# GpSimd's order in an attention kernel: first difference, store, spread, key weights, a lead-in piece and the last additions

## The chip, the cores and the metric

The kernel runs on one core of a Trainium2 chip. The metric is the device time of one execution in microseconds, the median of several. A profiled execution gives the trace; its times are counted from the start of the span.

## What is computed

`x` has 2048 rows of 256. It is normalised (layernorm), and two things are added to it: an attention with 16 heads of 128 and no mask, and a feed-forward part whose weights are rounded to -1, 0 and 1.

```
xn = layernorm(x)
q, k, v = split(xn @ Wqkv.T)                      # 16 heads of 128 each
w   = softmax(q @ k.T / sqrt(128))                # 2048 x 2048 for each head
att = concat_over_heads(w @ v) @ Wout.T
ffn = ((sigmoid(xn @ Q(w1).T) * (xn @ Q(w2).T)) @ Q(w3).T)
x + att + ffn
```

Everything is float32.

## The kernel before

**Blocks and steps.** Layernorm, the feed-forward part and the first projections come first, in about 105 us. Then the kernel goes through 64 blocks: a block `n` is a head `h` and 512 of its queries (`b` from 0 to 3). A block has four steps `t` of 128 queries each. One loop (`u`) emits all steps, with the order on every engine written out by hand (`manual_schedule`): each engine runs its own instructions strictly in the order in which the loop emits them. The step that makes the scores runs `LEAD` = 6 steps ahead: step `u` makes the scores of step `v = u + 6` and uses the weights of block `n`, step `t`. The first six steps (`u < 0`) are the lead-in; pieces of the projections of heads 0 and 1 are placed in it by the table `first`, whose key is `v`.

**One step.** TensorE makes the scores of 128 queries in two halves of 1024 keys, in three score buffers (`scores`). VectorE takes the maximum (`mx`, `nm`); ScalarE the exponential of both halves into `p`, of which there are four buffers. `exchanged` then sends `p` in 16 DMAs of 64 KB to `part`, ten issued by SyncE (SP) and six by ScalarE; each moves 32 rows. Two steps later VectorE turns `part` in 32 by 32 blocks into the big tile `R` (`transposed`, line 644), where the keys lie along the partitions. ScalarE issues the six DMAs between two pairs of exponentials.

**The product with the values.** `R` has seven slots of 2048 columns, and a block uses five of them under the names a, b, c, d, e (`roles`). The product of weights and values is done by a scheme with seven instead of eight multiplications: `differences` (line 664, GpSimd) makes T1 = c - a into e, T2 = d - e into a, T3 = c = d - c, T4 = b = b - a. T1 and T3 come in two halves (a, b), T2 in two halves of key tiles (l, h), and T4 whole. `weighted(n, t, k)` (line 711, TensorE, tile `av`) uses b and a as they are in step 0, T1 and T2 in step 1, T3 in step 2, T4 in step 3. T2 overwrites a, so it waits for step 0's products; step 1's products wait for T2. `v_combined` makes four combinations of the values on GpSimd for each head, two ahead of a head's first block and two within it. `copied` (ScalarE, line 729) and `added` (VectorE, line 737) bring the pieces together in `oU`. `added` and the second read of a projection are held back in the list `behind` and emitted at the start of the next step.

**The row sums.** `inverses(n + 1)` in step 2 of block `n` makes the reciprocals of the row sums on VectorE and stores them to the chip's main memory as `rd` (line 615, GpSimd's queue). `spread(n)` (line 621, GpSimd's queue) brings them back to all partitions as `oT`, 256 KB. `added(n, 3)` multiplies `oU` by `oT` (line 741), and `put_away(n)` (line 767, GpSimd's queue) stores `oU` to `od`; this is the store of the title.

**Other transfers on GpSimd's queue** (`between`). Heads go in pairs `g`, eight blocks `i` each. In the first three blocks of a pair (but the first pair) the output projection of the pair before is added into a running sum: `y_moved` fetches 512 KB of the sum (`osums<-yd`) at the end of step 0 and stores another 512 KB (`yd<-osums`) in step 3, and `o_fetched` fetches 512 KB (`o<-od`) at the end of step 1. The weights of the next pair are loaded by `load_weights` (line 83): query and key weights, 256 KB each, while the scores of an even head's last block are made, value weights in step 1 of a pair's fourth block. `weight_sums` makes four small sums of them on GpSimd.

**The end.** The last block has no steps of its own: `last_weighted` multiplies its weights directly, in two parts, and the last projections (`projected`, `opened`) stand between.

The step's order on GpSimd comes from these lines: in step 0 `put_away(n - 1)`, T1b, `spread(n)`, T3b, T2l and `between`; in step 1 T2h, two of `v_combined`, T4 and `between`; in step 3 T1a and T3a of the next block, with `y_moved` between them.

Of the kernel before, what the change touches and what calls it, by code (L numbers as in the profile page):

```python
# [20 lines left out]
def layernorm_attention_bitffn_kernel(  # L21
# [14 lines left out]
    nc = tc.nc  # L36
# [9 lines left out]
    TB = QB // P  # L46
# [4 lines left out]
    G = 2  # L51
# [21 lines left out]
    def load_weights(g: int, what: str, queue=nc.sync):  # L73

        if what == "o":
            w = wpool.tile([P, G, DM], F32, tag="wvo", name=f"wo{g}")
            src = woutT[g * G * D : (g + 1) * G * D, :].rearrange("(h p) e -> p h e", p=P)
        else:
            tag = "wvo" if what == "v" else f"w{what}"
            w = wpool.tile([P, KC, G * D], F32, tag=tag, name=f"w{what}{g}")  # L80
            lo = "qkv".index(what) * HD + g * G * D
            src = wqkvT[:, lo : lo + G * D].rearrange("(c p) e -> p c e", p=P)
        queue.dma_start(w, src)
        weights[g, what] = w
# [136 lines left out]
    NV = NKT // 2  # L221
# [395 lines left out]
    def spread(n: int):  # L617

        if n < NBK - NB:
            r = rds[n % 2].rearrange("(j c) r -> j (c r)", c=32)[:, : TB * 32]  # L620
            nc.gpsimd.dma_start(
                oT.rearrange("p (j x) -> p j x", j=P // 32), r.partition_broadcast(P)
            )
            rbs[n] = oT
# [24 lines left out]
    def differences(n: int, what: str):  # L649

        a, b, c, d, e = roles[n]
        todo, where = what[:2], what[2:]
        o, x, y = {"T1": (e, c, a), "T2": (a, d, e), "T3": (c, d, c), "T4": (b, b, a)}[todo]
        o, x, y = (R[:, i] for i in (o, x, y))
        if where in ("a", "b"):
            t = "ab".index(where)
            o, x, y = (i[:, t * S // 2 : (t + 1) * S // 2] for i in (o, x, y))
        elif where in ("l", "h"):
            k = "lh".index(where)
            o, x, y = (  # L660
                i.rearrange("p (t k q) -> p t k q", t=2 * NQ, q=32)[:, :, k * KH // 2 : (k + 1) * KH // 2]
                for i in (o, x, y)
            )
        nc.gpsimd.tensor_tensor(o, x, y, ALU.subtract)  # L664
# [99 lines left out]
    def put_away(n: int):  # L764

        h, b = blocks[n]
        nc.gpsimd.dma_start(ods[h // G % 2][b][:, h % G], oU)  # L767
# [60 lines left out]
    def projected(n: int, u: int, pool=ps_m, tag: str = "m"):  # L828
# [34 lines left out]

    first = {
        1: [("v", 0, NV - 1), ("k", 1, 0)], 2: [("k", 1, 1), ("q", 0, NB - 1)],
        3: [("k", 1, 2), ("q", 1, 1)], 4: [("k", 1, 3), ("q", 1, 2)], 5: [("v", 0, NV - 2)],
    }
    made = {("q", 1, 0)} | {p for todo in first.values() for p in todo}

# [28 lines left out]
    behind = []  # L898
    with tc.manual_schedule():
        for u in range(-LEAD, (NBK - 1) * TB):  # L900
            n, t = divmod(u, TB)
            v = u + LEAD
            lead_in = u < 0
            more = v < NBK * TB
            h, b = blocks[v // TB] if more else (H, 0)


            seven = 2 <= h + 1 < H and v % TB < 2
            hi = h + 1, b, v % TB
            product, read, twice = fast_product, fast_read, (b % 2, v % TB) != (1, 1)  # L910


            g, i = divmod(n, GB)
            if n >= NB and t < 2:
                i, j = divmod(i, NB)
                j = 2 * j + t
                if not i:
                    seven, hi = True, (g - 1, j)
                    product, read, twice = o_product, o_read, False
                elif g + 1 < H // G:  # L920
                    seven, hi = True, (g + 1, j)
                    product, read, twice = v_product, v_read, False
            pms = []

            def beside():
                if v == 0:

                    for c, f in chunks[-2:]:
                        summed(fp, c, f)
                if seven:  # L930
                    pms.append(product(*hi, False))
                    read(*hi, False, pms[0])

            if behind:
                behind.pop()()
            if t == 0 and n >= 0:
                if 0 < n <= NBK - NB:
                    put_away(n - 1)
                differences(n, "T1b")
                spread(n)  # L940
                differences(n, "T3b")
            elif t == 1 and n >= 0:
                differences(n, "T2h")
                if blocks[n][1] == 0:
                    v_combined(blocks[n][0], 2)
                    v_combined(blocks[n][0], 3)
                differences(n, "T4")
            elif t == 3 and -1 <= n < NBK - 2:
                differences(n + 1, "T1a")
                if n % GB < NB <= n < NBK - NB - 2:  # L950
                    y_moved(n % GB, True)
                differences(n + 1, "T3a")
                if n >= 0 and blocks[n + 1][1] == 0:
                    v_combined(blocks[n + 1][0], 0)
                    v_combined(blocks[n + 1][0], 1)
            if more:
                scores(v, late=beside)

            if lead_in:
                for what, hg, i in first.get(v, ()):  # L960
                    {"q": q_piece, "k": k_piece, "v": v_piece}[what](hg, i)
                if v == 1:
                    front.close()
                    apool = ctx.enter_context(tc.tile_pool(name="apool", bufs=2))
                    oT = apool.tile([P, QB], F32, tag="oT", name="oT", bufs=1)
                    oU = apool.tile([P, QB], F32, tag="oU", name="oU", bufs=1)
                    R = apool.tile([P, 7, S], F32, tag="R", name="R", bufs=1)
                    for c in range(0, NB, 2):
                        x_sums(c)
            elif t == 1 and n > NBK - NB:  # L970
                projected(n - 1, 0)
            if n >= NBK - NB and t in (0, 3):

                opened(n - NBK + NB, t // 3, *((ps_m, "m") if more else (ps_s, "s")))
            if h == 0:
                if v % TB == 0 and ("k", 1, b) not in made:
                    k_piece(1, b)
                elif v % TB == 1 and ("q", 1, b) not in made:
                    q_piece(1, b)
            if b == NB - 1 and h + 2 < H:  # L980
                if h % G == 0 and v % TB in (0, 2):
                    load_weights(h // G + 1, "qk"[v % TB // 2], nc.gpsimd)
                if v % TB == 3:
                    weight_sums(h + 2)
            twice = seven and twice
            if t == 2 and -1 <= n < NBK - 1:
                inverses(n + 1)
            if v > 1 and v - 2 < NBK * TB - 2:
                transposed(v - 2)
            if u >= 0:  # L990
                for k in range(units[t]):
                    weighted(n, t, k)
            if twice:
                pms.append(product(*hi, True))
            if u >= 0:
                copied(n, t)

            def left(n, t, twice, read, hi, h, b, v, product, pms, seven):
                if n >= 0:
                    added(n, t)  # L1000
                if twice:
                    read(*hi, True, pms[1])

            behind.append(partial(
                left, n, t, twice, read, hi, h, b, v, product, pms, seven
            ))
            if more:
                exchanged(v)
            if v == NBK * TB + 1:
                transposed(v - 3)  # L1010
                transposed(v - 2)
            if t == 2 and n > NBK - NB:
                projected(n - 1, 1)
            if u == -1:
                v_combined(0, 0)
                v_combined(0, 1)
            if u >= 0:
                if t == 0:
                    differences(n, "T2l")
                between(n, t)  # L1020

        n = NBK - 1
        behind.pop()()
        for k in range(NKT):
            last_weighted(k, 0)
            if k in (KQ - 1, 3 * KQ - 1):
                projected(n - 1, k // (2 * KQ), ps_s, "s")
            elif k == 2 * KQ - 1:
                opened(NB - 1, 0, ps_s, "s")
        for k in range(NKT):  # L1030
            last_weighted(k, 1)
            if k == KQ - 1:
                opened(NB - 1, 1, ps_s, "s")
                projected(n, 0, ps_m, "m")
        projected(n, 1, ps_s, "s")
# [38 lines left out]
```

## Time and profile before

| | us |
| --- | --- |
| median of 3 runs | 2227.57 |
| lowest, highest | 2225.85, 2231.21 |
| the profiled execution | 2229.07 |
| its span in the trace | 2227.3 |

| engine | busy us | what most of it is |
| --- | --- | --- |
| TensorE (PE) | 2178.7 | scores 936.2, products with values 541.2 and 476.5 |
| VectorE (DVE) | 1726.2 | maxima 619.6, transposes 605.3 |
| GpSimd (POOL) | 1471.9 | differences 1176.4 |
| ScalarE (ACT) | 744.0 | exponentials 565.8 |

| GpSimd's instruction | us on GpSimd | us from issue to landing, median |
| --- | --- | --- |
| half a difference, 128x1024 | 2.367 | |
| T4, 128x2048 | 4.545 | |
| a value combination, 128x512 | 1.28 | |
| spread `oT<-rd`, 256 KB | 0.778 | 5.6 |
| sums' store `od<-oU`, 256 KB | 0.568 | 3.1 |
| sum's fetch `osums<-yd`, 512 KB | 0.555 | 4.5 |
| o fetch `o<-od`, 512 KB | 0.571 | 4.6 |
| sum's store `yd<-osums`, 512 KB | 0.563 | 4.0 |
| key weights `wk`, 256 KB | 0.734 | 5.2 |

How to read the profile: PE is TensorE's matmul row, whose ends are modelled; PEld is its weight load; `ACTq` and `SPq` are DMA issues by ScalarE and SyncE. In the timeline a row has its start, its duration, the engine and line, the operation and its tiles, and in square brackets the engine's idle time before it and what ended that. Rows of the same kind are merged (x29 are 29 instructions). The windows view gives busy time of each engine in a stretch, and behind them the granted clock of TensorE (1.00 is full), the share of the DMA engines and GB/s.

### The profile page before, as it was taken

To read this page: it belongs to the slowest core of one execution; us is meant where nothing else is said; L and a number is where in the kernel's file an instruction comes from. 1 tells how busy PE (TensorE), PEld (TensorE's weight loads), DVE (VectorE), ACT (ScalarE), POOL (GpSimd) and SP (SyncE) were. 2 spreads that over 40 slices of the span, in tenths; PEclk is the share of its full clock that TensorE was granted. 3 is DMA by queue.
4 is the path that set the end of the run, shared out by engine and by line. 5 is a ranking of instruction groups with operands and counts; after the bars stand their busy time and mean duration, and the time that the engine had idled before them with its cause. 6 is when DMAs were issued, how large, how long until landed. Compare 5 with 4: busy or idle time off the path is not lost.

```text
span 2227.3 us, 41859 instructions
## 1 busy us (share of the span) xinstructions
PE 2178.7 (98%) x14074; PEld 1190.1 (53%) x14074; DVE 1726.2 (77%) x2338; ACT 744.0 (33%) x1390; POOL 1471.9 (66%) x884
## 2 busy tenths in 40 slices
PE   9999999999999999999999999999999999999998
PEld 6744545546665444445666444444454445665465
DVE  6567887877888788878788778877888878887774
ACT  5543333233333333323333233323333333332331
POOL 0067667867667776767677776677667668677662
PEclk9999999999999999999999999999999999999999
DMA  2166666776667766677667666677667776667763
GB/s 92 49 151 156 153 150 165 192 193 168 147 172 201 178 168 160 171 191 186 147 171 180 186 176 152 165 194 182 162 152 181 195 178 160 168 175 191 185 168 94
DMA packets 229928, 367.87 MB, mean 165 GB/s; under 512 B 70800, under 2 KB 76304, under 8 KB 229712
## 3 DMA queue, kind: packets, MB, share of 16 engines
q1 hardware_dynamic: 127664, 174.95, 30.5%
q10 hardware_dynamic: 74896, 101.94, 17.9%
q0 software_dynamic: 27152, 88.30, 16.7%
q8 instruction: 111, 1.82, 0.4%
q14 instruction: 105, 0.86, 0.1%
HBM read 61.93 MB, written 34.54 MB: 43 GB/s over the span
## 4 chain that ended last, share of the span: by engine, by line
PE 64%; DMA 14%; SPq 4%; POOL 4%; DVE 3%; issue 2%; ACT 2%; ACTq 1%; DVEq 0%
PE s L94 27%; PE av L711 24%; DMA part<-p 14%; PE pw L94 5%; PE pvw L94 4%; SPq L597 4%; POOL R L664 3%; PE pow L94 2%; ACT p L578 2%; ACTq L597 1%; DVE R L644 1%; DVE mx L568 1%; PE av L94 1%; DVE oU L741 1%; ACT oU L729 0%
## 5 line engine op out<-in xcount | busy, mean ns | idle before, releaser
L664 POOL TENSOR_TENSOR R<-R 128x1024 f32<-128x1024 f32 x441 | 1176.4, 2679 | 132.2 <-DVE R L644 91.0
L578 ACT ACTIVATE p<-s,nm 128x1024 f32<-128x1024 f32 x512 | 565.8, 1110 | 1343.8 <-DMA part<-p 958.6
L94 PE MATMUL s<-kT,qT 128*64 128x512 f32 x4000 | 936.2, 594 | 19.5 <-ACT p L578 19.4
L568 DVE TENSOR_REDUCE mx<-s 128x1 f32<-128x1024 f32 x512 | 619.6, 1222 | 292.9 <-PE s L94 279.6
L644 DVE STREAM_TRANSPOSE R<-part 128x1024 f32<-128x1024 f32 x512 | 605.3, 1220 | 40.8 <-DMA part<-p 37.3
L94 PEld LDWEIGHTS s<-kT,qT 128*64 128x64 f32 x4000 | 370.4, 137 | 455.6 <-issue 290.7
L711 PE MATMUL av<-R,v 128*64 128x256 f32 x3728 | 541.2, 380 | 0.1
L711 PE MATMUL av<-R,st 128*64 128x256 f32 x3024 | 476.5, 384 | 15.6 <-POOL R L664 12.3
L711 PEld LDWEIGHTS av<-R,v 128*64 128x64 f32 x3728 | 341.2, 137 | 164.4 <-issue 37.3
L711 PEld LDWEIGHTS av<-R,st 128*64 128x64 f32 x3024 | 296.9, 139 | 161.2 <-issue 38.2
L615 POOL DMA_DIRECT2D rd<-r x60 | 33.7, 562 | 234.2 <-DVE r L614 234.2
L767 POOL DMA_DIRECT2D od<-oU x60 | 34.1, 568 | 218.3 <-DVE oU L741 215.9
L737 DVE TENSOR_TENSOR oU<-av,oU 64x256 f32<-64x256 f32 x248 | 102.2, 412 | 68.0 <-ACT oU L729 65.6
L94 PE MATMUL pow<-o,wo 128*64 128x512 f32 x448 | 108.7, 593 | 3.5 <-DVE qT L197 3.4
L729 ACT COPY oU<-av 64x256 f32<-64x256 f32 x248 | 90.7, 366 | 62.2 <-PE av L711 58.3
L94 PE MATMUL pvw<-wv,xnT 128*64 128x256 f32 x896 | 110.6, 379 | 0.0
L578 ACT ACTIVATION_READ_ACCUMULATOR p<-s,nm 128x1 f32 x512 | 100.3, 196 | 0.0
L94 PE MATMUL pw<-t,ws 128*64 128x512 f32 x336 | 98.0, 592 | 0.0
L94 PEld LDWEIGHTS pvw<-wv,xnT 128*64 128x64 f32 x896 | 69.7, 137 | 50.9 <-issue 16.0
L200 DVE TENSOR_TENSOR kT<-pw,kT 128x512 f32<-128x512 f32 x112 | 76.9, 686 | 1.8
L160 POOL TENSOR_TENSOR t<-xnT 128x512 f32<-128x512 f32 x4 | 5.1, 1267 | 106.8 <-DMA part<-p 106.8
L94 PEld LDWEIGHTS pow<-o,wo 128*64 128x64 f32 x448 | 38.3, 137 | 62.5 <-issue 43.0
(145 smaller groups left out, 1302.6 us busy)
## 6 DMA issues: line engine op xcount, KB each, us to landing
part<-p SPq DMA_DIRECT2D x2556, 64.0 KB, 2.3
part<-p ACTq DMA_DIRECT2D x1540, 64.0 KB, 2.3
oT<-rd POOLq DMA_DIRECT2D x60, 256.0 KB, 5.6
od<-oU POOLq DMA_DIRECT2D x60, 256.0 KB, 3.1
o<-od POOLq DMA_DIRECT2D x28, 512.0 KB, 4.6
osums<-yd POOLq DMA_DIRECT2D x28, 512.0 KB, 4.5
yd<-osums POOLq DMA_DIRECT2D x26, 512.0 KB, 4.0
yd<-yT SPq DMA_DIRECT2D x4, 512.0 KB, 2.6
```

The lines of the kernel that those rows point to most:

```text
L94: nc.tensor.matmul(out[c * HP : (c + 1) * HP], lhs[:, c * HP : (c + 1) * HP], rhs, start=start, stop=stop, skip_group_check=True,)
L200: nc.vector.tensor_tensor(k, pk, base, ALU.add)
L568: nc.vector.tensor_reduce(mx[:, i : i + 1], s, AX.X, ALU.max)
L578: nc.scalar.activation(p, s, AF.Exp, bias=nm, scale=SCALE, accum_out=sums[n][:, t, i : i + 1],)
L597: queue.dma_start(parts[v][g // 2][bass.ts(j, 32), g % 2, :], ps[j // 2][bass.ts(g, 32), bass.ts(j % 2, S // NQ)],)
L615: nc.gpsimd.dma_start(rds[n % 2], riT)
L644: nc.vector.transpose(to[:, t % 2, 2 * i : 2 * i + 2], part.rearrange("p g (s c) -> p g s c", s=2),)
L664: nc.gpsimd.tensor_tensor(o, x, y, ALU.subtract)
L711: nc.tensor.matmul(av[i * HP : (i + 1) * HP, half], l[:, kk], moving(s, kk), start=start, stop=(k == units[r] - 1), skip_group_check=True,)
L729: nc.scalar.copy(u[op, oq], av[ap, half])
L737: nc.vector.tensor_tensor(u[p, q], av[p, half], u[p, q], ALU.add)
L767: nc.gpsimd.dma_start(ods[h // G % 2][b][:, h % G], oU)
```

## The change

Five edits, all of them in the order in which instructions are emitted; no instruction is added or removed.

1. T1b is emitted ahead of `put_away(n - 1)` instead of behind it.
2. `spread(n)` moves from step 0, between T1b and T3b, to step 1, behind T2h. In the pair's first three blocks the sum's fetch, at the end of step 0, now comes ahead of it, and the o fetch, at the end of step 1, still behind it.
3. The next pair's key weights are loaded one step of `v` earlier: behind T3a in step 3, where before they stood behind T3b in step 0 of the next block. The query weights stay.
4. In the lead-in the last v piece goes from `v` = 5 to 4 and the last k piece from 4 to 5.
5. The additions of the last full step (`added(62, 3)`) are emitted ahead of the last four transposes on VectorE instead of behind them.

GpSimd's order of a block is then T1a, T3a | T1b, store, T3b, T2l | T2h, spread, T4.

```diff
     first = {
         1: [("v", 0, NV - 1), ("k", 1, 0)], 2: [("k", 1, 1), ("q", 0, NB - 1)],
-        3: [("k", 1, 2), ("q", 1, 1)], 4: [("k", 1, 3), ("q", 1, 2)], 5: [("v", 0, NV - 2)],
+        3: [("k", 1, 2), ("q", 1, 1)], 4: [("v", 0, NV - 2), ("q", 1, 2)], 5: [("k", 1, 3)],
     }
...
             if t == 0 and n >= 0:
+                differences(n, "T1b")
                 if 0 < n <= NBK - NB:
                     put_away(n - 1)
-                differences(n, "T1b")
-                spread(n)
                 differences(n, "T3b")
             elif t == 1 and n >= 0:
                 differences(n, "T2h")
+                spread(n)
...
             if b == NB - 1 and h + 2 < H:
-                if h % G == 0 and v % TB in (0, 2):
-                    load_weights(h // G + 1, "qk"[v % TB // 2], nc.gpsimd)
+                if h % G == 0 and v % TB in (0, 1):
+                    load_weights(h // G + 1, "qk"[v % TB], nc.gpsimd)
...
             if v == NBK * TB + 1:
+                behind.pop()()
                 transposed(v - 3)
                 transposed(v - 2)
...
         n = NBK - 1
-        behind.pop()()
         for k in range(NKT):
```

## The prediction

> **What bounds the kernel now.** I read the page first, then who waited for whom, then the timeline at each place where TensorE stood idle. The page says which engine sets the time:
>
> ```profile
> PE 2178.7 (98%) x14074; PEld 1190.1 (53%) x14074; DVE 1726.2 (77%) x2338; ACT 744.0 (33%) x1390; POOL 1471.9 (66%) x884
> ```
>
> TensorE (PE) is the bound. GpSimd (POOL) is busy two thirds of the time, so reordering it pays only where PE stands still for it. The view of waits, PE alone, gives those places (us, times, longest):
>
> ```profile
> PE s L94 <- ACT p L578: 19.4, 21, 3.1
> PE av L711 <- POOL R L664: 12.3, 12, 2.8
> ```
>
> Twelve waits for a difference, 12.3 us, are what this order can remove. The 19.4 us are scores that wait for a score buffer which ScalarE frees late; those are the danger. The timeline around block 0, then block 2, shows two of the twelve (start, duration, engine, line, idle before and its releaser):
>
> ```profile
> 141.37 1.27 POOL L686 TENSOR_TENSOR st<-v 128x512 f32<-128x512 f32 x1 [2.60 <-ACT v L242]
> 146.26 0.78 POOL L621 DMA_DIRECT2D oT<-rd  x1
> 151.78 5.14 PE L711 MATMUL av<-R,st 128*64 128x256 f32 x29 [2.55 <-POOL R L664]
> ...
> 205.41 0.58 POOL L767 DMA_DIRECT2D od<-oU  x1 [0.84 <-DVE oU L741]
> 211.43 0.73 POOL L83 DMA_DIRECT2D wk<-in_wqkvT_dram  x1
> 212.18 9.26 POOL L664 TENSOR_TENSOR R<-R 128x1024 f32<-128x1024 f32 x3
> 214.59 6.35 PE L711 MATMUL av<-R,st 128*64 128x256 f32 x29 [2.85 <-POOL R L664]
> ```
>
> PE waits for T2 in both, and the matmuls after the wait run slowly: 29 took 5.14 and 6.35 us, where elsewhere 32 take 3.45 us, that is 3.13 for 29. The windows view gives the reason (the column after POOL is the granted clock):
>
> ```profile
> 152.00:156.00 4.00, 4.00 (x24) 2.34 (x22) 2.37 (x2) 1.93 (x3) 4.00 (x3) 0.57 0.58 142
> ```
>
> A wait of 2.55 us is paid for again in clock. A steady block, then the first heavy block of a pair of heads, where the key weights come in between:
>
> ```profile
> 1023.79 0.58 POOL L767 DMA_DIRECT2D od<-oU  x1 [3.90 <-DVE oU L741]
> 1026.69 0.78 POOL L621 DMA_DIRECT2D oT<-rd  x1
> 1027.49 11.64 POOL L664 TENSOR_TENSOR R<-R 128x1024 f32<-128x1024 f32 x4
> ...
> 997.87 0.73 POOL L83 DMA_DIRECT2D wk<-in_wqkvT_dram  x1
> 1003.95 0.44 PE L711 MATMUL av<-R,st 128*64 128x256 f32 x2 [0.60 <-POOL R L664]
> ```
>
> In a steady block GpSimd idles 3.90 us, then stores, takes T1b, the spread, T3b and both T2 halves in one go, and PE (from 1034.75) just finds them ready. One more issue of 0.73 us in that run costs PE 0.60. Last, the tail:
>
> ```profile
> 2197.41 4.62 DVE L644 STREAM_TRANSPOSE R<-part 128x1024 f32<-128x1024 f32 x4
> 2202.06 0.43 DVE L737 TENSOR_TENSOR oU<-av,oU 64x256 f32<-64x256 f32 x1
> 2202.54 1.08 PE L94 MATMUL po<-wo,oU 128*64 128x256 f32 x8 [2.00 <-DVE oU L737]
> 2203.45 3.44 PE L94 MATMUL av<-R,v 128*64 128x256 f32 x16
> ```
>
> Four transposes stand ahead of an addition that PE waits for; then 16 matmuls take 3.44 instead of 1.72 us.
>
> **How much earlier T2 comes in a block.** Two moves: T1b goes ahead of the store, the spread goes behind T2h. T1b cannot use all of the 3.90 us: it needs the transposes of the block's last step, which DVE ends at 1022.31 (1019.95 + 2.36). So T1b runs 1022.35 to 1024.7, the store follows to 1025.3 (0.9 later than before; it landed after 3.1 us, median, and ScalarE overwrites oU only at 1030.01, so this is hidden with 1.6 us to spare, and costs at most that excess), T3b to 1027.65. Before, T3b ended at 29.85. Gain 2.2 us: 0.78 of spread and 1.4 of T1b. T2l then also waits for the first products, which read what it overwrites (PE from 1026.15, half through at about 1028.1), so 1.7 of the 2.2 are left here. The spread has most of a block until DVE multiplies by it: no cost there.
>
> **The terms, one for each stall.**
> 1. Block 0. The v piece in step 4 instead of 5 puts its ScalarE copies at about 135 instead of 141, so the first v combination follows T3a at 138.8 instead of 141.37: 2.6 us, and 0.78 for the spread. T2l ends at about 148.5 instead of 151.7, T2h at 150.8, where PE wants its fifth tile at 150.4. Of 2.55 idle and 5.14 - 3.13 = 2.0 of clock some 0.35 stays: **4.2**. The key piece that moves the other way, one PE run of 1.88 us, is needed ten steps later: 0.
> 2. Block 1. Idle 1.72 and 0.35 (181.63, 183.93). Transposes end at 171.4, so T1b to 173.8, store, T3b to 176.7, T2l to 179.05; PE is there at 179.3: **2.0**.
> 3. Block 2. GpSimd is late because the query weights waited until 198.41; that is unchanged. The key weights stay ahead of T2, as they now stand ahead of T1b. T1b 205.3 to 207.65, T3b to 210.55, T2l to 212.9 instead of 214.5: 1.6 of 2.85. With 1.3 us left I take the clock as kept, since the 1.72 of block 1 cost none: 6.35 - 3.13 = 3.2 more. **4.8** (1.6 if the clock still falls).
> 4. Block 3. 0.32 and 0.35, T2 comes 2.2 earlier: **0.65**.
> 5. Five waits like the one at 1003.95, 0.6 each: T2h comes 0.73 earlier by the weights and 1.7 by the rest: **3.0**.
> 6. Block 60. 1.08 at 2121.34; no spread there, but T1b moves out from behind the store: **1.1**.
> 7. Tail. The addition needs ScalarE's copy (2198.85 + 0.36), ends at 2199.7, PE comes at 2200.4: 2.00 idle and 3.44 - 1.72 of clock, **3.7**. The transposes end 2.4 later, at 2204.4; their reader, the second half of the last block, starts after 2211: hidden.
>
> Sum 19.4.
>
> The Trainium skill (TensorE: Matmul & The Clock Gate, section Why this matters for your kernels) advises "No PE-idle gaps >~3µs between matmul bursts" against a fall to half rate. By that rule waits of 2.55, 2.85 and 2.00 us cost no clock, and the sum would be 12.5. The trace shows 0.57 of the clock after the first of them, so I keep the clock terms.
>
> **What the moved transfers cost.** ScalarE issues six exchange DMAs a step between exponentials, and GpSimd's transfers hold that up:
>
> ```profile
> 990.01 4.04 ACTq L597 DMA_DIRECT2D part<-p  x6
> 996.61 6.14 ACTq L597 DMA_DIRECT2D part<-p  x6
> 1003.00 1.11 ACT L578 ACTIVATE p<-s,nm 128x1024 f32<-128x1024 f32 x1 [6.03 <-DMA part<-p]
> ```
>
> Six issues take 4.04 us alone and 6.14 with spread and key weights under way. In light blocks the spread delays the exponentials of the step after it by 0.5 to 3.5 us (their start behind the end of the negated maximum) and PE stays busy all the time (131.00 of 131 us in 533 to 664), so a spread one step later delays another step by as much: 0. In heavy blocks (the first three of a pair of heads, seven pairs) a sums' fetch precedes it and an o fetch follows. Before: spread 958.40, fetch 963.84, o fetch 971.36 and query weights. After, by the rows: fetch about 962.3, spread 965.3, o fetch 970.6. The exponentials at 970.30 gain the spread of before and lose that of after, and those at 980.39 see the same sum of transfers: 0, between -1 and +1 for each pair, so -7 to +7.
>
> The key weights now go out after T3a, about 985 in this pair, into six issues that already took 4.9 us beside the sums' store, and just ahead of a PE wait of 1.06 (at 988.94). They add at least 0 (if they fall beside exponentials) and at most their own 1.6; in return they leave the next block's spread and fetch. Nearest row: 6.14 - 4.04 = 2.1 for spread and weights together, so half of that, less what comes back: 0.5 net in six pairs, **-3**. On GpSimd they stand ahead of T1b and wait for the step's last key product, which ends before T3a does.
>
> 19.4 - 3 = 16.4 us. The profiled execution took 2229.07 (span 2227.3 and 1.8 around it), 1.5 above the median 2227.57. So 2212.7 for that run, and 2211.2 for the median.
>
> **Rivals.**
> - Given back (0.13): PE comes 16 us earlier only to meet ScalarE; block 0 to 2 exponentials were themselves 2.7 to 3.5 us behind their maxima at the stalls. Terms 1 to 3 then shrink to half, -5.5, and the transfers cost 5 more: about 2222 to 2231. Against it: their lateness came from the spread that also moves.
> - Slower (0.12): the row of transfers. Fetch, spread and o fetch now lie within 9 us instead of 14 in each of 21 heavy blocks. If the exponentials come over about 4 us late (5.2 behind gave the stall at 980), each adds 2 us idle, the size of one spread's delay: 42 against 19, about 2250, and more where the clock falls. It decides from 0.9 us a heavy block on.
> - Relief (0.13): the heavy blocks' spread no longer meets the exponentials that are already late, and of the 19.4 us for ACT p and the 3.4 us that the stall of 3.12 us before 2068.19 cost in clock (0.50 in the window 2068 to 2072) half goes, or all: 2200 to 2188.
>
> The Trainium skill (DMA: Bandwidth & Descriptors, section Queues, rings and completion order) says that each engine goes round-robin between queues packet by packet. By that a moved spread takes only its share anywhere, and the slower rival has no price of its own; the 6.14 against 4.04 shows more than nothing.
>
> **How the numbers follow.** Forecast 0.62, with 2203 to 2220; relief 0.13, given back 0.13, slower 0.12. About 0.3% (6.7 us) is what a measurement can tell: faster 0.75, same 0.13, slower 0.12. Eight in ten: from within relief, 2196, to given back's end, 2231.
>
> **What would show it.** Right: waits of PE for POOL R fall from 12.3 to about 2 us; no reduced clock near 152, 215 and 2204; no wait at `po`; PE's wait for ACT p stays near 19. Wrong: that last wait grows over 27 us, with ACTq runs of 7 us behind the spread, or the waits for R remain because T1b ends no sooner.

## The result, and the profile after

| | before | after |
| --- | --- | --- |
| median, us | 2226.90 (6 runs, 2224.36 to 2236.21) | 2256.55 (6 runs, 2245.31 to 2261.36) |
| profiled execution, us | 2229.07 | 2258.29 |
| its span, us | 2227.3 | 2256.5 |

The changed kernel is slower: its time is 1.0120 times that of before, 95% interval [1.0089, 1.0151]. The page, the busy time of the engines:

```profile
PE 2173.6 (96%) x14074; PEld 1066.7 (47%) x14074; DVE 1784.4 (79%) x2338; ACT 744.6 (33%) x1390; POOL 1475.9 (65%) x884
```

PE did its work in 5 us less and was idle for longer. VectorE (DVE) is busy 58 us longer with the same 2338 instructions: something there became slow. Who waited for whom, PE alone (waiting tile and line, releaser, us, times, longest):

```profile
PE s L94 <- ACT p L578: 27.7, 33, 3.0
PE pvw L94 <- DVE qT L197: 18.2, 14, 1.5
PE pow L94 <- DVE qT L197: 17.7, 13, 1.5
PE av L711 <- ACT oU L729: 5.1, 1, 5.1
```

The line `av <- POOL R`, 12.3 us before, is gone: what the change was to remove, it removed. In its place stand 27 waits of about 1.3 us (35.9 us; 3.4 before) for line 197, `q_sum`, VectorE's second read of a projection out of PE's only projection bank, and 8 us more for ScalarE's exponentials. Over all rows of this view PE's waits rose from 45.1 to 78.9 us. Against that, the time lost to a clock of 0.5 (half of the time spent at it, counted by me over the trace after 50 us) fell from 14.5 to 4.7. That makes +24.0 of the +29.2 us in the span; the other 5 us I have not placed.

What became slow on VectorE is one line. The product of `oU` and the reciprocals, first of before, then of after (tile `oT`; times in ns: shortest, median, longest; and the first and last start):

```profile
L741 DVE TENSOR_TENSOR oU<-oU,oT 128x512 f32<-128x512 f32 x60 | 44.0, 734 | 2.1
```

```profile
L741 DVE TENSOR_TENSOR oU<-oU,oT x60: 691/2210/2882, 169.9 to 2139.5; 128x512 f32<-128x512 f32 x60
```

From 44.0 to 106.7 us (60 times 1778 ns): 62.7 us more, which covers the extra time of VectorE as a whole. The timeline of a light block of after shows why:

```profile
566.04 2.36 POOL L664 TENSOR_TENSOR R<-R 128x1024 f32<-128x1024 f32 x1 [2.92 <-DVE R L644]
566.45 2.49 DVE L741 TENSOR_TENSOR oU<-oU,oT 128x512 f32<-128x512 f32 x1
568.98 0.69 DVE L197 TENSOR_TENSOR qT<-pw,qT 128x512 f32<-128x512 f32 x1
569.24 0.56 POOL L767 DMA_DIRECT2D od<-oU  x1 [0.84 <-DVE oU L741]
569.72 1.95 PE L94 MATMUL pvw<-wv,xnT 128*64 128x256 f32 x16 [1.28 <-DVE qT L197]
```

T1b starts 0.41 us ahead of the product, which now lasts 2.49 instead of 0.69 us and ends at 568.94, 0.54 after T1b's end at 568.40. In this trace 49 of the 60 products start over 0.03 us before the end of a GpSimd difference or combination, and every one of them ends 0.55 to 0.56 us behind that instruction, however long the two lie side by side. So the product does not run slowly beside GpSimd: it stands until GpSimd is done. Line 197 comes behind it, frees the bank 1.8 us later than with a product of 0.69, and PE waits 1.28 us.

The hold works in the other direction too: a GpSimd half that starts 0.3 us behind a running product takes 2.81 us instead of 2.36. The transposes (line 644, one input) are not held: their median is 1.23 us beside GpSimd's arithmetic and 1.20 without it.

The Trainium skill has this rule (SBUF — State Buffer, section SBUF: two separate sides): VectorE and GpSimd share one pair of ports (SBUF is the chip's big on-chip memory), which a VectorE instruction with two inputs in SBUF and a GpSimd instruction that reads SBUF take as a whole; the later one "fully blocks". The end of the product, always 0.55 us behind GpSimd's, agrees. Line 741 has both inputs in SBUF. Line 737 takes one of its two from PSUM, the memory that the matmuls write: 232 of its 248 instructions on `oU` run beside GpSimd's arithmetic, with a median of 0.42 us, and the 16 others take 0.43.

The gain that was forecast is in the same trace. The windows view, in blocks 0 and 2 and at the tail, which in this trace lies 31 us later (the column after POOL is the granted clock):

```profile
148.00:156.00 8.00, 7.98 (x54) 4.36 (x52) 6.17 (x7) 3.03 (x6) 7.98 (x6) 1.00 0.80 167
208.00:216.00 8.00, 7.07 (x48) 4.31 (x50) 6.53 (x8) 4.18 (x8) 7.98 (x5) 1.00 0.67 133
2230.00:2240.00 10.00, 10.00 (x102) 8.23 (x104) 7.14 (x9) 0.37 (x1) 0.66 (x2) 1.00 0.25 78
```

In the first PE stands still for 0.02 us where the wait of 2.55 us was, in the second for 0.93, for ScalarE and no longer for a difference, and in the third not at all. The clock is full in all three.

### The profile page after: what moved, and what is told of

It is laid out like the page before. It is cut to its first block, busy times and chain, and to the rows that moved or that the text cites. A ratio compares the mean times of both kernels' runs of the same rounds, so it can differ in the third digit from the quotient of the medians.

```text
span 2256.5 us, 41871 instructions
## 1 busy us (share of the span) xinstructions
PE 2173.6 (96%) x14074; PEld 1066.7 (47%) x14074; DVE 1784.4 (79%) x2338; ACT 744.6 (33%) x1390; POOL 1475.9 (65%) x884
## 4 chain that ended last, share of the span: by engine, by line
PE 50%; DMA 22%; DVE 10%; SPq 8%; ACT 4%; issue 4%; ACTq 2%; DVEq 0%
DMA part<-p 22%; PE av L711 17%; PE s L94 17%; SPq L597 8%; PE pvw L94 4%; DVE R L644 3%; ACT p L578 3%; PE pow L94 3%; ACTq L597 2%; DVE oU L741 2%; PE pw L94 2%; PE ph L446 2%; DVE mx L568 2%; DVE oU L737 1%; PE pf L469 1%
## 5 line engine op out<-in xcount | busy, mean ns | idle before, releaser
L94 PE MATMUL s<-kT,qT 128*64 128x512 f32 x4000 | 912.1, 594 | 27.9 <-ACT p L578 27.7
L94 PEld LDWEIGHTS s<-kT,qT 128*64 128x64 f32 x4000 | 287.0, 137 | 539.0 <-issue 422.7
L711 PE MATMUL av<-R,v 128*64 128x256 f32 x3728 | 528.5, 379 | 2.7 <-DVE oU L737 1.3
L711 PE MATMUL av<-R,st 128*64 128x256 f32 x3024 | 458.8, 380 | 5.4 <-ACT oU L729 5.1
L711 PEld LDWEIGHTS av<-R,v 128*64 128x64 f32 x3728 | 326.0, 137 | 144.2 <-issue 48.8
L711 PEld LDWEIGHTS av<-R,st 128*64 128x64 f32 x3024 | 285.1, 137 | 189.8 <-issue 50.9
L741 DVE TENSOR_TENSOR oU<-oU,oT 128x512 f32<-128x512 f32 x60 | 106.7, 1778 | 2.1
L94 PEld LDWEIGHTS pvw<-wv,xnT 128*64 128x64 f32 x896 | 63.0, 137 | 78.8 <-DVE qT L197 30.5
L94 PE MATMUL pw<-t,ws 128*64 128x512 f32 x336 | 86.7, 593 | 1.2 <-DVE kT L200 1.1
L94 PEld LDWEIGHTS pow<-o,wo 128*64 128x64 f32 x448 | 31.0, 137 | 85.8 <-issue 56.0
```

What stands on the lines that cost most here:

```text
L94: nc.tensor.matmul(out[c * HP : (c + 1) * HP], lhs[:, c * HP : (c + 1) * HP], rhs, start=start, stop=stop, skip_group_check=True,)
L711: nc.tensor.matmul(av[i * HP : (i + 1) * HP, half], l[:, kk], moving(s, kk), start=start, stop=(k == units[r] - 1), skip_group_check=True,)
L741: nc.vector.tensor_tensor(u, u, r, ALU.mult)
```

## The experiments

The kernel before had medians of 2221 to 2223 us beside these runs and 2227 beside the first; so kernels are compared by their ratios to it, with 95% intervals.

The first question was whether T1b beside the product (edit 1) is the whole loss, through line 197 and the single bank, or whether the moved transfers (edits 2 and 3) make ScalarE late, as the slower rival had it.

**Edit 1 undone, and edit 1 alone.** `t1b_back` is the changed kernel with

```
                 if 0 < n <= NBK - NB:
                     put_away(n - 1)
+                differences(n, "T1b")
                 differences(n, "T3b")
```

and without the T1b ahead of it; `t1b_only` is the kernel before with edit 1 and nothing else.

> The changed kernel with edit 1 alone undone: the store stands ahead of T1b again, the spread stays behind T2h, the other edits stay. Theory A: VectorE's product with the reciprocals (line 741) is held until GpSimd's T1b, which now runs beside it, has ended; that makes the second read of the projections late (qT, line 197), and TensorE waits for it. Then line 741 falls from a median of 2.21 us back to 0.69, the waits of PE pvw and PE pow for DVE qT fall from 35.9 to about 3 us, and the time from 2256 to 2215 to 2226. Theory B: the moved spread and key weights make the loss through late exponentials. Then the waits for ACT p stay at 25 us or more and the time stays above 2245.

> The kernel before with edit 1 alone: T1b ahead of the store, spread between store and T3b as before. Theory A: line 741 rises to a median over 2 us, PE's waits for DVE qT to 30 us or more, waits for POOL R fall below 12.3, time 2245 to 2260. Theory B: T1b is harmless, time 2215 to 2230.

Measured: `t1b_back` 2191.08 us, ratio to before 0.9862 [0.9840, 0.9885]; `t1b_only` 2257.87, 1.0161 [1.0137, 1.0185]. Edit 1 by itself costs 36 us; without it the other four edits gain 31. On top of those four it costs 57 (1.0120 less 0.9862, of 2221). That rules out theory B, which wanted 2245 or more without edit 1; and 2191 lies 24 us below the range of theory A. PE's waits in `t1b_only`, then in `t1b_back`:

```profile
PE s L94 <- ACT p L578: 24.1, 26, 2.9
PE pvw L94 <- DVE qT L197: 18.2, 14, 1.5
PE pow L94 <- DVE qT L197: 17.6, 13, 1.5
```

```profile
PE s L94 <- ACT p L578: 8.6, 9, 2.6
PE pow L94 <- DVE qT L197: 4.6, 4, 1.5
PE av L711 <- POOL R L664: 3.5, 5, 1.4
```

The 27 waits for line 197 come with edit 1, and 6 (6.2 us) are left without it (the median of line 741 is 2491 ns in the one, 693 in the other). But edit 1's price on the other edits is larger than those 36 us: the wait for the exponentials falls to 8.6 us as well, which the first theory does not say. And what edit 1 was to buy is small: with T1b behind the store PE's waits for differences are 3.5 us instead of 12.3, so most of that gain needs no edit 1.

**Three ways to keep T1b first and spare PE.** `read_first` takes the product out of `added` into `multiplied` and emits it behind the second read:

```
                     read(*hi, True, pms[1])
+                if n >= 0 and t == 3:
+                    multiplied(n)
```

`t1b_quarters` cuts T1b in two differences of 512 columns, each emitted in its turn. `mult_gpsimd` moves the product to GpSimd, between T1b and the store:

```
                 if 0 < n <= NBK - NB:
+                    multiplied(n - 1)
                     put_away(n - 1)
...
-            nc.vector.tensor_tensor(u, u, r, ALU.mult)
+            nc.gpsimd.tensor_tensor(u, u, r, ALU.mult)
```

> The changed kernel with one thing more: VectorE makes the second read of the projection (qT, line 197) ahead of the product with the reciprocals instead of behind it. Theory A in full: line 741 is still held by T1b (median 2 us or more), but nobody waits for it in the projections' buffer: PE's waits for DVE qT fall from 35.9 to under 5 us and the time to 2220 to 2230. If the product's delay hurts by the maxima that stand behind it on VectorE instead, the waits for qT go and waits for ACT p grow by as much, time 2240 to 2256. Theory B: no change, 2250 or more.

> The changed kernel with T1b cut in two instructions of 128x512, one after the other, in the same place. Theory A1: the two engines exclude each other for one instruction at a time. Then line 741 can go between the two pieces: its median falls from 2.2 to 1.0 to 1.5 us, the waits for DVE qT from 35.9 to under 15, time 2205 to 2235. Theory A2: VectorE is held as long as GpSimd has such work. Then line 741 stays over 2.2 us and the time over 2248.

> The changed kernel with the product with the reciprocals on GpSimd, behind T1b and ahead of the store, instead of on VectorE (60 products of 128x512, about 1.28 us each by the value combinations). Theory A: nothing on VectorE has two inputs in the big memory beside T1b any more, PE's waits for DVE qT fall under 4 us; T2 comes 1.3 us later than in the changed kernel, still about 0.4 to 0.9 ahead of the kernel before; time 2212 to 2226. Theory B: 2245 or more.

Measured: `read_first` 2222.46, 1.0005 [0.9986, 1.0023]; `t1b_quarters` 2224.11, 1.0010 [0.9991, 1.0029]; `mult_gpsimd` 2196.97, 0.9891 [0.9870, 0.9911]. The waits of `read_first`:

```profile
PE s L94 <- ACT p L578: 28.1, 31, 1.9
PE pow L94 <- DVE qT L197: 4.8, 7, 0.7
```

With the read ahead of the held product the 35.9 us for line 197 are 5.2 (0.4 of it at `pvw`), and the kernel is 26 us faster than after (1.0120 less 1.0005). So the chain product, read, bank, PE is shown; but it is only about half of edit 1's price. The product itself is still held, but for less (median 1.57 us). The wait for ScalarE stays at 28.1 us.

In `t1b_quarters` the two pieces start each behind its own transpose, and the product meets the second alone:

```profile
557.63 2.52 POOL L667 TENSOR_TENSOR R<-R 128x512 f32<-128x512 f32 x2 [1.79 <-DVE R L644]
559.17 1.52 DVE L744 TENSOR_TENSOR oU<-oU,oT 128x512 f32<-128x512 f32 x1
561.47 1.95 PE L94 MATMUL pvw<-wv,xnT 128*64 128x256 f32 x16 [0.31 <-DVE qT L197]
```

The product ends at 560.69, again 0.54 us behind GpSimd's end at 560.15. It lasts 1.52, and PE waits 0.31: the hold is for the one GpSimd instruction that is running, so a shorter one holds for less. All waits for line 197 come to 13.7 us. In `mult_gpsimd` nothing is held: the product takes 1.27 us on GpSimd, the waits for line 197 are 0.7 us, and those for the exponentials 12.1; its time is 15 us below the range that was expected.

**The other edits taken apart.** `spread_only` is the kernel before with `spread(n)` moved behind T2h (edit 2); `rest_only` has edits 3, 4 and 5 and the order of before in steps 0 and 1. `spread_after_t4` is `t1b_back` with

```
                 differences(n, "T2h")
-                spread(n)
...
                 differences(n, "T4")
+                spread(n)
```

> The kernel before with edit 2 alone: the spread moved behind T2h, all else as it was. Theory C: with the store ahead of T1b the changed order gained 30 us, more than the waits for T2 are worth, because the moved spread no longer holds up the exponentials. Then this edit alone takes the waits for ACT p from 19.4 to 8 to 12 us and the time from 2221 to 2200 to 2207 (some of it from T2 coming 0.78 earlier). Theory D: the relief comes from the key weights, the lead-in and the tail. Then ACT p stays at 17 or more and the time at 2214 to 2221.

> The kernel before with edits 3, 4 and 5 (key weights, lead-in piece, last additions) and without edits 1 and 2. Theory C: these are worth their places only: about 2.6 of block 0's 2.55 us idle with its clock, 0.6 in each of some pairs, 3.7 in the tail, so 2208 to 2215, with ACT p between 15 and 22. Theory D: 2205 or less with ACT p at 12 or less. If the key weights hurt as the prediction had it, ACT p rises over 22 and the time stays over 2216.

> The store ahead of T1b (edit 1 undone, the rest of the change kept), and the spread behind T4 instead of behind T2h, some 4.5 us later in the same step. T2 comes exactly as early as with the spread behind T2h. Theory C: what counts is that the spread's transfer falls beside ScalarE's exponentials and its wait for TensorE, and not beside its six exchange DMAs. Behind T4 it falls on those of step 1: waits for ACT p rise from 8.6 to 15 to 27 us, time 2197 to 2215. Rival E: it only has to be out of the way of T2. Then ACT p stays under 12 and the time at 2188 to 2195.

Measured: `spread_only` 2200.60, 0.9901 [0.9874, 0.9929]; `rest_only` 2215.54, 0.9978 [0.9961, 0.9995]; `spread_after_t4` 2250.26, 1.0129 [1.0107, 1.0152]. PE's wait for the exponentials in the three, in this order:

```profile
PE s L94 <- ACT p L578: 9.6, 8, 3.3
```

```profile
PE s L94 <- ACT p L578: 26.7, 23, 4.7
```

```profile
PE s L94 <- ACT p L578: 36.8, 23, 4.9
```

The spread's place is the largest gain in the change, 22 us alone; nearly half of that shows in the wait for the exponentials, 9.6 us after 19.4. The waits for differences fall by 5.7 us, as T2 comes earlier, and the time lost at half clock by 6.7. One T4 of 4.5 us further on, behind it, the spread loses 59 us against `t1b_back`, far more than theory C had (its 2197 to 2215 became 2250): 28 us are waits for the exponentials, 7 for line 197, and 14 are lost at half clock (16.7 after 2.5). So the 256 KB are not free, and their place decides. A light block of before, then of `t1b_back` (ACTq is ScalarE's issue of the exchange):

```profile
1091.20 0.78 POOL L621 DMA_DIRECT2D oT<-rd  x1
1091.35 1.11 ACT L578 ACTIVATE p<-s,nm 128x1024 f32<-128x1024 f32 x1 [4.60 <-DMA part<-p]
1094.64 6.24 ACTq L597 DMA_DIRECT2D part<-p  x6
```

```profile
1054.69 0.79 POOL L621 DMA_DIRECT2D oT<-rd  x1
1058.49 0.36 ACT L729 COPY oU<-av 64x256 f32<-64x256 f32 x1 [1.32 <-PE av L711]
1058.57 0.51 ACTq L597 DMA_DIRECT2D part<-p  x1
1059.13 3.67 ACTq L597 DMA_DIRECT2D part<-p  x5
```

Before, the six issues that follow the spread's issue took 6.24 us. In `t1b_back` ScalarE first makes the exponentials and then waits 1.32 us for PE, while the spread passes, and its six issues take 4.23 us (1058.57 to 1062.80). Over the 29 light blocks from 12 to 57 (worked out from the trace, first to last of six issues, mean), with the step that the spread falls on in bold:

| | step 0 | step 1 | step 2 | step 3 |
| --- | --- | --- | --- | --- |
| before | **5.83** | 4.54 | 4.25 | 4.30 |
| `t1b_back` | 4.32 | **4.79** | 4.28 | 4.26 |
| `spread_after_t4` | 4.45 | **6.08** | 4.77 | 4.27 |

Against some 4.3 us in a step without it, the same transfer adds 1.5 us, 0.5 us or 1.8 us to ScalarE's issues, by where it is issued: 0.1 us before the start of step 0's exponentials, 1.2 before that of step 1's, 3.6 behind it (medians of the same blocks).

The Trainium skill states that each DMA engine goes round-robin between queues (DMA: Bandwidth & Descriptors, section Queues, rings and completion order). The prediction drew from it that a moved spread has no price of its own; that inference does not hold here, where the place alone made 59 us.

**Key weights, and the fastest order.** `back_weights_late` is `t1b_back` with the weights where they were (`v % TB in (0, 2)`); `back_read_first` is `t1b_back` with the second read ahead of the product; `read_first_late` is both.

> The store ahead of T1b and the key weights back at their old place, behind T3b in step 0 (edits 1 and 3 undone, 2, 4 and 5 kept). Theory F: the early key weights cost exponentials, as ACT p rose from 19.4 to 26.7 us where edits 3 to 5 stood alone: ACT p falls from 8.6 to under 6, while T2 is late by 0.73 again in one block of each pair, which costs under 1 us; time 2183 to 2190. Rival: with the spread out of the way the place of the key weights is worth nothing, or T2 pays for it: 2190 to 2196.

> The store ahead of T1b (edit 1 undone, the rest of the change kept), and VectorE's second read of the projection ahead of the product with the reciprocals. The waits for DVE qT, 6.2 us with the store ahead, go to under 2; the store follows 0.7 later and T1b with it, which may bring up to 3 us of waits for POOL R. Theory A: 2185 to 2190. If the product behind the read meets a difference again, line 741 rises over 1 us in its median and the time is over 2195.

> All that helped together: store ahead of T1b, spread behind T2h, lead-in piece and last additions moved, the projection's second read ahead of the product with the reciprocals, and the key weights at their old place. Theory F: 2179 to 2187. If the place of the key weights is worth nothing, 2185 to 2190.

Measured: `back_weights_late` 2195.36, 0.9868 [0.9846, 0.9889]; `back_read_first` 2187.62, 0.9846 [0.9817, 0.9876]; `read_first_late` 2190.22, 0.9864 [0.9844, 0.9884]. Each pair lies within the other's interval: with the spread moved, the weights' place is worth nothing that these runs can tell. With the spread in its old place `rest_only` has 26.7 us of waits for the exponentials against 19.4, though that kernel as a whole is 5 us faster; it carries edits 3, 4 and 5 together, so whether the key weights make that wait is not shown. `back_read_first` is the fastest order found, 1.5% faster than before and 2.7% faster than the changed kernel; its lead on `t1b_back` is within the intervals.

**The second half of edit 1's price.** With the read ahead of the product T1b first still costs 35 us (`read_first` less `back_read_first`, 1.0005 less 0.9846). Either the held product still did it, or the earlier transfers did: with T1b first, the sum's fetch and the spread come about 1.9 us earlier beside step 0's exponentials. `no_product` is the changed kernel without line 741, so that the sums stay unscaled; `no_product_back` is the same of `t1b_back`.

> The changed kernel without the product with the reciprocals (line 741 left out, so the sums stay unscaled); T1b stays ahead of the store. Nothing is left for T1b to hold up. The first half of edit 1's cost, the waits for DVE qT, goes as in the run with the second read first. What of the other half? Theory G: T1b ahead of the store brings T2, and with it the sum's fetch and the spread, some 1.9 us nearer to the exponentials of step 0, onto ScalarE's exchange DMAs. Then ACT p stays at 20 to 30 us and the time at 2205 to 2225. Theory H: the second half also comes from VectorE being held (later maxima). Then ACT p falls under 14 and the time to 2175 to 2195.

> The same without the product, with the store ahead of T1b (edit 1 undone): the control for the run without the product. Theory G: ACT p 5 to 12 us, time 2180 to 2192, at least 20 below that run. Theory H: both within 8 us of each other.

Measured: `no_product` 2211.89, 0.9951 [0.9934, 0.9967]; `no_product_back` 2202.73, 0.9912 [0.9890, 0.9934]. Their waits, in this order:

```profile
PE s L94 <- ACT p L578: 27.5, 28, 2.4
```

```profile
PE s L94 <- ACT p L578: 18.9, 18, 3.8
```

With nothing to hold, the changed kernel's wait for the exponentials is still 27.5 us, so the hold is not its cause. `mult_gpsimd` differs from `no_product` only by 1.27 us of GpSimd's work ahead of the store: it does more and takes 13 us less (0.9951 less 0.9891), with 12.1 us of waits instead of 27.5. Those 1.27 us move all of GpSimd's work behind them, the sum's fetch and the spread with it. In a heavy block of after, then of `t1b_back`:

```profile
1010.42 0.56 POOL L779 DMA_DIRECT2D osums<-yd  x1
1013.30 0.79 POOL L621 DMA_DIRECT2D oT<-rd  x1
1010.14 7.03 ACTq L597 DMA_DIRECT2D part<-p  x6
1017.43 1.11 ACT L578 ACTIVATE p<-s,nm 128x1024 f32<-128x1024 f32 x1 [6.92 <-DMA part<-p]
```

```profile
986.05 0.56 POOL L779 DMA_DIRECT2D osums<-yd  x1
988.94 0.79 POOL L621 DMA_DIRECT2D oT<-rd  x1
984.53 5.39 ACTq L597 DMA_DIRECT2D part<-p  x6
990.18 1.12 ACT L578 ACTIVATE p<-s,nm 128x1024 f32<-128x1024 f32 x1 [5.29 <-DMA part<-p]
```

In after the fetch goes out with the first of six issues, the spread follows 2.9 us later, and the six take 7.03 us; in `t1b_back` the fetch comes 1.5 us behind the first issue, and the six take 5.39. Over the 20 heavy blocks from 8 to 57 (worked out from the traces): the sum's fetch, counted from the start of step 0's exponentials (median); the six issues of steps 0 and 1 (means); how late step 2's exponentials start, counted from the end of `nm` (mean); and PE's whole wait for exponentials. In order of the fetch:

| | fetch after | step 0's six issues | step 1's six issues | step 2's exponentials late by | PE's wait |
| --- | --- | --- | --- | --- | --- |
| `read_first` | 2.81 | 6.47 | 6.52 | 3.90 | 28.1 |
| after | 2.82 | 5.98 | 6.63 | 3.72 | 27.7 |
| `no_product` | 3.50 | 6.04 | 6.76 | 3.42 | 27.5 |
| `t1b_quarters` | 3.54 | 5.85 | 6.68 | 3.21 | 19.5 |
| `no_product_back` | 4.36 | 4.79 | 6.66 | 2.42 | 18.9 |
| `t1b_back` | 4.67 | 4.05 | 5.06 | 1.05 | 8.6 |
| `mult_gpsimd` | 5.09 | 4.28 | 5.46 | 1.47 | 12.1 |
| before | 5.84 | 6.26 | 5.79 | 2.60 | 19.4 |

`spread_only`, `back_read_first`, `back_weights_late` and `read_first_late` have the fetch at 5.3, 1.2 to 1.5 us of lateness and waits of 5.9 to 11.2 us. Before stands apart: there the spread, and not the fetch, goes out with step 0's exponentials (0.16 us behind their start, median). In the others a fetch before 3.6 goes with exponentials 3.2 to 3.9 us late, and one at 4.6 or later with 1.0 to 1.5, whether a product is held (`read_first`) or there is none (`no_product`).

So the transfers' time, not the hold, goes with the second half. Its size is not settled. T1b first costs 57 us in the kernel as it is, 35 with the read first, and 9 with no product at all. The last pair was expected 20 us or more apart, and 9 is nearly the 8 that theory H allowed; but `no_product_back` is itself slower than `t1b_back`, its wait 18.9 us after 8.6, its fetch and spread coming earlier too. No run holds the transfers' times fixed while T1b moves, so that they cause this half is argued, from `mult_gpsimd` against `no_product` and from the table.

## Why the prediction was wrong, point by point

**The step that failed: T1b in the free stretch.** "So T1b runs 1022.35 to 1024.7, the store follows" gave T1b a price of nothing on VectorE. The gap of 3.90 us was free on GpSimd, but not beside it: VectorE's product lies in it, and PE stands behind the read that follows the product. The trace of before had the sign. In its block 2 GpSimd happened to be late, and the product ran into a pair of halves:

```profile
199.72 4.84 POOL L664 TENSOR_TENSOR R<-R 128x1024 f32<-128x1024 f32 x2
203.03 2.09 DVE L741 TENSOR_TENSOR oU<-oU,oT 128x512 f32<-128x512 f32 x1
```

2.09 us against 0.69, ending 0.56 us behind GpSimd. It is the one row of sixty so long (seven more took 0.74 to 0.89, behind a value combination), and the group's mean of 734 ns hid it. By it the product that starts at 1022.80, within the T1b that was forecast for 1022.35 to 1024.7, would have stood until about 1025.26: 1.8 us of hold in a light block. 27 waits of 1.3 us came of it, 35.9 us or twice the whole forecast gain. None of the rivals had this mechanism.

**Terms 1 to 6** held in the waits: for a difference PE waits no more, and the clock at blocks 0 and 2 is full. A clock lost behind a wait of 2.55 us and kept without it also bears out counting the clock terms; of the 14.5 us lost at half clock, 9.8 came back. By the same count the three stretches of before near 152, 214 and 2204 lost 1.7, 3.4 and 1.7 us, where the terms had 2.0, 3.2 and 1.7.

**Term 7** held at its place, no wait at `po` and the clock at 1.00. Some 11 us ahead of it, in step 2 of block 62, PE waits 5.1 us for ScalarE's copy, 3.2 before; `t1b_only`, without edit 5, has 4.1 there and `t1b_back`, with it, 1.1, so this is not given back by the tail's edit.

```profile
2222.00 0.69 PE L711 MATMUL av<-R,st 128*64 128x256 f32 x1 [5.12 <-ACT oU L729]
```

**The spread at 0, from -7 to +7,** was mis-sized: alone it gains 22 us. "A spread one step later delays another step by as much" is the sentence that failed: 1.5 us of delay became 0.5, in light blocks too. The relief rival had the mechanism (most of the waits for the exponentials go), and its 2200 to 2188 holds the four edits without T1b (0.9862 of 2227 is 2196).

**The key weights at -3** are not seen: no difference between `t1b_back` and `back_weights_late`. The rows behind this term were read too simply: the 4.04 us were not taken alone, since the sums' store goes out within them (991.86), and the 6.14 us have the sum's fetch (1000.93) beside the key weights.

**The slower rival** named transfers that lie closer and make ScalarE late. Its signs, a wait over 27 us and ACTq runs of 7 us, are there (27.7; 7.03), but not by edit 2, which alone gains; they come with T1b first, which brings fetch and spread out 1.9 us sooner. That its 2250 lies near the 2257 measured is luck: the largest part of the loss, the waits for line 197, was not in it. What a badly placed spread can cost shows with the spread behind T4: 59 us.

**In one sum:** the four other edits gain 31 us instead of the 16 forecast for all five; T1b first costs 57, about 26 of it by the held product and the late read; the rest goes with the transfers that come earlier; that they cause it is argued, not shown.

## What to carry to other kernels

A stretch in which an engine is idle is free for it alone: before putting work there, list what the other engines run in the same microseconds, and look for an instruction of theirs whose longest time is far above its median: here that one row had the price of the overlap. Then follow who stands behind the instruction that would be slowed; here reading the projection bank ahead of the held product took 26 us back although the product was still held (median 1.57 us). And a DMA that is moved is not priced by its bytes: measure what the other queue's issues take at its old and new phase.

## What was not expected of the hardware

- A VectorE product of two SBUF tensors of 128x512 stood for as long as a GpSimd difference ran and ended 0.55 us after it, whether that difference took 2.36 us or 1.28; a transpose, or an addition with one input in PSUM, was not touched.
- 256 KB issued by GpSimd made ScalarE's six issues of 64 KB 0.5 or 1.8 us longer, by when they were issued; between these two places the kernel's time differs by 59 us in 2190.
